# Linear attention with two chunks per step, and the state sums of a chunk as one product

## Chip, cores and metric

The kernel runs on one NeuronCore of a Trainium2 chip. The metric is the device time of one execution in microseconds (us), and the lower one is better. Five queues work beside each other on the core: TensorE (PE in the profile; its weight loads are PEld), VectorE (DVE), ScalarE (ACT), GpSimd (POOL), and SyncE (SP), which here only issues transfers. Each queue takes its instructions in a fixed order, so an instruction that waits holds up all that stand behind it on its queue.

## The reference

A layer of two parts over x with 2048 tokens of width 512, all in float32.

```python
x = x + attn(layernorm(x), Wq, Wk, Wv, Wo)        # 16 query heads, 4 key/value heads, head width 128
x = x + moe(layernorm(x), w_cls, bias, w_gate_up, w_down)   # 64 scores, 8 picked, 32 real experts

# attn: rotary embedding on q and k, then qf = elu(q) + 1, kf = elu(k) + 1, and per head, token by token:
state = state + kf[:, None] * v[None, :]          # 128 x 128
z     = z + kf
out   = (qf @ state) / (qf @ z + 1e-6)
```

The attention is linear: a running 128x128 sum `state` per key/value head takes the place of a softmax over all earlier tokens. The change lies in this part alone, and in the memory that it uses.

## The kernel before, in words

**Tiling.** The 2048 tokens are four blocks (`sb`) of 512; a block has four chunks (`c`) of P = 128 tokens, and a chunk two halves (`a`) of T = 64. There are G = 4 groups (`g`), one for each key/value head, with R = 4 query heads each. Inside a half, attention is computed as masked scores times values; what came earlier enters through the running state, which is therefore needed at the start of each half.

**A block.** `norm_block` normalises the 512 tokens and transposes them to `xT`. `values` makes v for each chunk (L271, one 128x512 PSUM tile, copied by ACT at L274). `project(sb, g)` makes k (L305) and four q (L317) for a group. `rope_feature` (L282 to L288) turns each 128x512 PSUM tile into features: six VectorE instructions and one exponential on ACT. `project` also makes the denominators: a running sum of k (L309), four products with q (`qz`, L325), 16 small matmuls (`pd`, L328), a reciprocal (L331, L332). The reciprocal row is stored to DRAM (L333) and read back once per chunk as `rds`, spread over all 128 partitions (L337, 256 KB per chunk, 512-byte pieces). `by_token` transposes k of the group to `kk` (L294).

**`attend(sb, g, c)`** works on one chunk:
- the scores of both halves (L355): each fills 64 of the 128 PSUM partitions, shown as tile 128*64;
- the sums of k times v (L361), twice: over the first half alone (64 rows, tile 64*128), and over the whole chunk (128*128);
- VectorE adds both to the old state (L366) and masks the scores (`at`, L370);
- for each half, state times q (L376, 128*128) and values times masked scores (L379, 64 rows, 64*128) go into one PSUM tile `po`, one bank for each half;
- VectorE multiplies `po` by `rds` into `oT` (L381).

When group 3 of a block is reached, `output` multiplies `oT` of all 16 heads by Wo, chunk by chunk (`px`, L391), and `route` and `list_further` pick experts for the finished tokens. The second part, the experts, begins after the last block.

**Order.** The loop at the end of the attention writes, for each group, first `project` of the next group and then `attend` of this one, four chunks. A scheduler then places the instructions on each queue, so work of two groups is mixed. It keeps the data dependencies and the limits of the pools: two PSUM buffers `p_pj` for k, q, v and output products; two buffers `p_sc` for scores and sums; one buffer for each `po`; three for `rds` (`rdp`); two for the rotary tables `cs` and `sn` (`blk`), of which the next block's pair is loaded one block ahead; one value tile `va` per chunk.

These are the lines that set how far ahead a reciprocal can be read back, with the names used below:

```python
rdp = ph.enter_context(tc.tile_pool(name="rdp", bufs=NC - 1))      # NC = 4
...
for c in range(NC):
    t = rdp.tile([P, R, P], F32, tag="rds", name=f"rds_{sb}_{g}_{c}")
    nc.sync.dma_start(out=t, in_=recip[sb][g][:, c, :].unsqueeze(0).to_broadcast([P, R, P]))
```

Of the kernel before, what the change touches and what calls it, by code (L numbers as in the profile page):

```python
# [9 lines left out]
F32 = mybir.dt.float32  # L10
# [3 lines left out]
ALU = mybir.AluOpType  # L14
AX = mybir.AxisListType
PSUM = bass.MemoryType.PSUM
DRAM = bass.MemoryType.DRAM

P = 128
# [3 lines left out]
G = 4  # L23
R = H // G
# [28 lines left out]
def linattn_moe(  # L53
# [121 lines left out]

    with ExitStack() as ph:
        wts = ph.enter_context(tc.tile_pool(name="wts", bufs=1))
        blk = ph.enter_context(tc.tile_pool(name="blk", bufs=2))
        xnp = ph.enter_context(tc.tile_pool(name="xnp", bufs=1))
        qkp = ph.enter_context(tc.tile_pool(name="qkp", bufs=2))  # L180
        zp = ph.enter_context(tc.tile_pool(name="zp", bufs=1))
        rdp = ph.enter_context(tc.tile_pool(name="rdp", bufs=NC - 1))
        rowp = ph.enter_context(tc.tile_pool(name="rowp", bufs=NC))
        vap = ph.enter_context(tc.tile_pool(name="vap", bufs=NC))
        otp = ph.enter_context(tc.tile_pool(name="otp", bufs=G))
        stp = ph.enter_context(tc.tile_pool(name="stp", bufs=2))
        tmp = ph.enter_context(tc.tile_pool(name="tmp", bufs=2))
        sml = ph.enter_context(tc.tile_pool(name="sml", bufs=2))
        p_tr = ph.enter_context(tc.tile_pool(name="p_tr", bufs=1, space=PSUM))
        p_pj = ph.enter_context(tc.tile_pool(name="p_pj", bufs=2, space=PSUM))  # L190
        p_sc = ph.enter_context(tc.tile_pool(name="p_sc", bufs=2, space=PSUM))
        p_o = ph.enter_context(tc.tile_pool(name="p_o", bufs=1, space=PSUM))
        p_ms = ph.enter_context(tc.tile_pool(name="p_ms", bufs=1, space=PSUM))

# [50 lines left out]
        def norm_block(sb):  # L245
# [17 lines left out]
                nc.scalar.copy(xT[:, :, ts(c, P)], pt)  # L263
            return xT

        def values(sb, c, xT):

            pv = p_pj.tile([P, G, HD], F32, tag="pj", name=f"pv_{sb}_{c}")
            pvf = pv.rearrange("p g d -> p (g d)")
            for k in range(KD):  # L270
                nc.tensor.matmul(pvf, lhsT=xT[:, k, ts(c, P)], rhs=wv[:, k, :],  # L271
                                 start=(k == 0), stop=(k == KD - 1))
            va = vap.tile([P, G, HD], F32, tag="va", name=f"va_{sb}_{c}")
            nc.scalar.copy(va, pv)  # L274
            return va

        def rope_feature(dst, ps, sb, name):

# [61 lines left out]

        state = [None] * G

        def attend(sb, g, c, proj, kk, va, oT):


            kT, qT, rds = proj
            n = f"{sb}_{g}_{c}"
            halves = range(P // T)
            half = [slice(c * P + a * T, c * P + (a + 1) * T) for a in halves]
            old = state[g]  # L350
            psk = p_sc.tile([P, R * T + 2 * HD], F32, tag="sc", name=f"psk_{n}")
            psc = psk[:, : R * T].rearrange("p (r t) -> p r t", r=R)
            pst = psk[:, R * T :].rearrange("p (a d) -> p a d", a=2)
            for a in halves:
                nc.tensor.matmul(psc[ts(a, T)], lhsT=kT[:, half[a]], rhs=qT[:, :, half[a]],  # L355
                                 start=True, stop=True)

            n_new = 2 if sb < NSB - 1 or c < NC - 1 else 1
            for a in range(n_new):
                to = slice(0, (a + 1) * T)  # L360
                nc.tensor.matmul(pst[:, a], lhsT=kk[to, c], rhs=va[to, g, :], start=True, stop=True)  # L361
            new = stp.tile([P, 2, HD], F32, tag=f"st{g}", name=f"state_{n}")
            if old is None:
                nc.vector.tensor_copy(new, pst)
            else:
                nc.vector.tensor_tensor(new[:, :n_new], pst[:, :n_new],  # L366
                                        old[:, 1:].to_broadcast([P, n_new, HD]), ALU.add)
            state[g] = new
            at = tmp.tile([P, R, T], F32, tag="at", name=f"at_{n}")
            nc.vector.tensor_tensor(at, psc, causal.unsqueeze(1).to_broadcast([P, R, T]), ALU.mult)  # L370
            pos = []
            for a in halves:
                po = p_o.tile([P, R, T], F32, tag=f"o{a}", name=f"po_{n}_{a}")
                before_half = (old[:, 1] if old is not None else None, new[:, 0])[a]
                if before_half is not None:
                    nc.tensor.matmul(po, lhsT=before_half, rhs=qT[:, :, half[a]], start=True, stop=False)  # L376
                pos.append((po, before_half is None))
            for a, (po, first) in enumerate(pos):
                nc.tensor.matmul(po, lhsT=va[ts(a, T), g, :], rhs=at[ts(a, T)], start=first, stop=True)  # L379
            for a, (po, first) in enumerate(pos):  # L380
                nc.vector.tensor_tensor(oT[:, :, half[a]], po, rds[c][:, :, ts(a, T)], ALU.mult)  # L381

        def output(sb, c, oTs, between=None):

# [19 lines left out]
        def route(ch, xw):  # L404
# [16 lines left out]
            nc.vector.reciprocal(sm, sm)  # L421
            nc.vector.tensor_scalar(sc, sc, sm, None, ALU.mult)

            sb_ = sml.tile([P, EZ], F32, tag="sbias", name=f"sbias_{ch}")
            nc.vector.tensor_tensor(sb_, sc, bias_r, ALU.add)
            t8 = sml.tile([P, TOPK], F32, tag="t8", name=f"t8_{ch}")
            nc.vector.max(out=t8, in_=sb_)
            rest = sml.tile([P, EZ], F32, tag="rest", name=f"rest_{ch}")
            nc.vector.match_replace(out=rest, in_to_replace=t8, in_values=sb_, imm_value=-3.0e38)
            sel = sml.tile([P, EZ], F32, tag="sel", name=f"sel_{ch}")  # L430
            nc.vector.tensor_tensor(sel, sb_, rest, ALU.not_equal)
# [18 lines left out]
            nc.vector.tensor_copy(pos, pp)  # L450
            if ch >= LISTED:

                free = sml.tile([P, E], F32, tag="hi", name=f"free_{ch}")
                nc.vector.tensor_scalar(free, sel[:, :E], -float(NONE), float(NONE), ALU.mult, ALU.add)
                nc.vector.tensor_tensor(free, pos, free, ALU.add)
                here = tmp.tile([P, E, SL], BF16, tag="rb", name=f"here_{ch}")
                ph_ = p_ms.tile([P, NQ, 2], F32, tag="ms", name=f"ph_{ch}")
                for i in range(2):
                    es = slice(i * E // 2, (i + 1) * E // 2)
                    nc.vector.tensor_tensor(here[:, es],  # L460
                                            free[:, es].unsqueeze(2).to_broadcast([P, E // 2, SL]),
                                            places.unsqueeze(1).to_broadcast([P, E // 2, SL]), ALU.is_equal)
                    for q in range(i * NQ // 2, (i + 1) * NQ // 2):
                        nc.tensor.matmul(ph_[:, q, :],
                                         lhsT=here[:, Q * q : Q * (q + 1), :].rearrange("p e s -> p (e s)"),
                                         rhs=tok2[:, ch, :], start=True, stop=True)
                nc.vector.tensor_tensor(held, held, ph_, ALU.add)

            hi = sml.tile([P, E], F32, tag="hi", name=f"hi_{ch}")
            nc.vector.tensor_scalar(hi, pos, float(C2), float(P * NCOL - 1), ALU.is_ge, ALU.mult)  # L470
            mi = sml.tile([P, E], F32, tag="mi", name=f"mi_{ch}")
            nc.vector.scalar_tensor_tensor(mi, pos, float(SL), off_2, ALU.is_ge, ALU.mult)
            ad = sml.tile([P, E], F32, tag="ad", name=f"ad_{ch}")
            nc.vector.scalar_tensor_tensor(ad, pos, -float(NCOL), off_e, ALU.mult, ALU.add)
            nc.vector.tensor_tensor(hi, hi, mi, ALU.add)
            nc.vector.tensor_tensor(ad, ad, hi, ALU.add)
            ok = sml.tile([P, E], F32, tag="ok", name=f"ok_{ch}")
            nc.vector.scalar_tensor_tensor(ok, pos, float(CAP), sel[:, :E], ALU.is_lt, ALU.mult)
            nc.vector.tensor_tensor(ad, ad, ok, ALU.mult)
            a8 = sml.tile([P, TOPK], F32, tag="a8", name=f"a8_{ch}")  # L480
# [20 lines left out]
        for sb in range(NSB):  # L501
# [2 lines left out]
                blocks[sb + 1] = load_block(sb + 1)  # L504
            for g in range(G):
                if g == 0:
                    vas = [values(sb, c, xTs[sb]) for c in range(NC)]
                if g + 1 < G:
                    projs[sb, g + 1] = project(sb, g + 1, xTs[sb])
                elif not last:  # L510
                    xTs[sb + 1] = norm_block(sb + 1)
                    projs[sb + 1, 0] = project(sb + 1, 0, xTs[sb + 1])
                if last and g == G - 1:
                    for i in range(2):
                        load_pair(i)
                oT = otp.tile([P, R, SB], F32, tag="oT", name=f"oT_{sb}_{g}")
                oTs[sb, g] = oT
                kk = by_token(sb, g, projs[sb, g][0])
                for c in range(NC):
                    attend(sb, g, c, projs[sb, g], kk, vas[c], oT)  # L520
                    if g == G - 1:
                        if c != 1 and waiting:
                            route_and_list(*waiting.pop(0))
                        if c >= 1:
                            waiting.append((sb * NC + c - 1,
                                            output(sb, c - 1, [oTs[sb, i] for i in range(G)])))
# [20 lines left out]

        pc = p_ms.tile([P, E], F32, tag="ms", name="pc")
        nc.tensor.matmul(pc, lhsT=ones, rhs=selcum, start=True, stop=True)
        big = sml.tile([P, 2, 2, E // 2], F32, tag="big", name="big")  # L550
        for i, n in enumerate((SL, C2)):
            nc.vector.tensor_scalar(big[:, i].rearrange("p a b -> p (a b)"), pc, float(n) + 0.5, None,
                                    ALU.is_ge)
# [296 lines left out]
```

## Time and profile before

| | us |
|---|---|
| median of 3 runs (lowest, highest) | 1238.45 (1237.87, 1241.02) |
| the profiled execution, whole | 1237.05 |
| its span, first to last instruction | 1235.3 |
| PE busy in the span | 1050.5 (85%) |
| DVE busy | 637.9 (52%) |
| ACT, POOL busy | 130.2, 219.7 |
| PE clock granted, mean | 0.933 |

The attention takes about the first 900 us. A block has a stage of values and the first `project` (33.3 us in the second block), two stages of `attend` beside `project` (33.7 and 33.3), a third with the next block's normalisation (35.8), and one with the last group and the output products (80.7). The rest of the span is the experts. These stages run from the first `values` product (L271) or the first transposes of `by_token` (L294) of a group to those of the next. A share of busy time is a mean over stages, so the stages are looked at one by one.

### The profile page before, as it was taken

How to read it: one execution, taken by the hardware profiler on the slowest of the kernel's cores; microseconds unless marked ns; L12 is line 12 of the kernel's file. 1: busy time of each engine (PE TensorE's matmuls, PEld its weight loads, DVE VectorE, ACT ScalarE, POOL GpSimd, SP SyncE). 2: the span in 40 equal slices, each digit the busy share in tenths (PEclk: the TensorE clock that was granted, in tenths of full speed). 3: DMA queues.
4: the chain of work that ended last, by engine and by line, in shares of the span. 5: the costliest groups of instructions: out<-in, count | busy, mean ns of one | idle time of the engine just before them, and what ended most of it. 6: DMA issues, size and time to landing. Idle time of an engine off the chain costs nothing. (4 is left out here: it accounts for less than half of the span.)

```text
span 1235.3 us, 13580 instructions
## 1 busy us (share of the span) xinstructions
PE 1050.5 (85%) x4410; PEld 530.9 (43%) x4410; DVE 637.9 (52%) x1553; ACT 130.2 (11%) x256; POOL 219.7 (18%) x254
## 2 busy tenths in 40 slices
PE   5999999999999899999999999999737765672772
PEld 2444444444444444444444444444312554441440
DVE  4888874358888435888843388834322111110110
ACT  1111110011121001112100111100011100110000
POOL 4000001430000343000034200023353121211211
PEclk9999999999999999999999999999967877786887
DMA  9411212100121210012321112340572484967224
GB/s 346 151 16 33 69 49 55 52 26 13 34 77 40 60 52 27 13 35 58 75 61 52 61 45 67 102 59 27 167 254 74 109 273 149 319 187 235 45 39 156
DMA packets 90840, 116.26 MB, mean 94 GB/s; under 512 B 12493, under 2 KB 47309, under 8 KB 90672
## 3 DMA queue, kind: packets, MB, share of 16 engines
q1 hardware_dynamic: 74640, 93.53, 25.5%
q0 software_dynamic: 10336, 12.51, 5.2%
q10 hardware_dynamic: 5760, 8.92, 2.0%
q8 instruction: 55, 0.90, 0.3%
q14 instruction: 49, 0.40, 0.1%
HBM read 101.35 MB, written 20.96 MB: 99 GB/s over the span
## 5 line engine op out<-in xcount | busy, mean ns | idle before, releaser
L317 PE MATMUL pq<-xT,wq 128*128 128x512 f32 x512 | 230.3, 599 | 10.1 <-DVE rb_q L284 10.1
L391 PE MATMUL px<-wo,oT 128*128 128x512 f32 x512 | 232.4, 599 | 0.0
L166 POOL DMA_INDIRECT slots<-tok,ai x120 | 117.6, 980 | 501.5 <-DVE ai L485 468.9
L317 PEld LDWEIGHTS pq<-xT,wq 128*128 128x128 f32 x512 | 94.4, 190 | 138.5 <-issue 107.3
L391 PEld LDWEIGHTS px<-wo,oT 128*128 128x128 f32 x512 | 93.9, 191 | 98.1 <-issue 97.6
L728 PE MATMUL pu<-xeT,gu 128*128 128x224 f32 (+1 forms) x352 | 69.4, 367 | 11.0 <-DVE xeT L656 9.7
L376 PE MATMUL po<-qT,state 128*128 128x256 f32 x248 | 76.8, 402 | 2.2 <-DVE oT L381 1.9
L728 PEld LDWEIGHTS pu<-xeT,gu 128*128 128x128 f32 x352 | 65.4, 230 | 15.4 <-issue 13.1
L393 DVE TENSOR_TENSOR x<-px,x 128x512 f32<-128x512 f32 x16 | 11.1, 692 | 113.6 <-PE px L391 98.8
L381 DVE TENSOR_TENSOR oT<-po,rds 128x256 f32<-128x256 f32 x128 | 50.1, 414 | 33.7 <-PE po L379 18.8
L305 PE MATMUL pk<-xT,wk 128*128 128x512 f32 x128 | 63.5, 627 | 0.7 <-ACT xT L263 0.7
L242 POOL TENSOR_TENSOR lnr<-lnv,mhalf 128x1 f32<-128x1 f32 (+1 forms) x20 | 13.3, 664 | 255.0 <-DVE lnv L240 228.8
L271 PE MATMUL pv<-wv,xT 128*128 128x512 f32 x128 | 57.7, 598 | 0.0
L361 PE MATMUL psk<-va,kk 64*128 64x128 f32 (+1 forms) x248 | 56.7, 323 | 0.0
L287 ACT ACTIVATE rb_q<-rb_q 128x512 f32<-128x512 f32 x64 | 40.3, 630 | 155.4 <-DVE rb_q L286 155.1
L376 PEld LDWEIGHTS po<-qT,state 128*128 128x128 f32 x248 | 41.2, 189 | 35.6 <-issue 21.7
L379 PE MATMUL po<-at,va 64*128 64x256 f32 x256 | 54.6, 428 | 0.0
L355 PE MATMUL psk<-qT,kT 128*64 128x256 f32 x256 | 50.5, 404 | 0.0
L361 PEld LDWEIGHTS psk<-va,kk 64*128 64x128 f32 (+1 forms) x248 | 36.8, 186 | 31.6 <-issue 23.8
L643 POOL DMA_INDIRECT acc<-y,idx x17 | 25.9, 1524 | 130.0 <-ACTq L778 40.0
L672 PE MATMUL pu_b<-gu,xeT_b 128*32 128x256 f32 x512 | 40.2, 424 | 10.0 <-issue 9.5
L325 DVE TENSOR_TENSOR qz<-qT,zT 128x512 f32<-128x512 f32 x64 | 42.4, 687 | 11.1 <-PE pd L328 10.6
(180 smaller groups left out, 1135.1 us busy)
## 6 DMA issues: line engine op xcount, KB each, us to landing
gu<-in_wgu_dram SPq DMA_DIRECT2D x32, 1024.0 KB
rds<-recip SPq DMA_DIRECT2D x64, 256.0 KB
dn<-in_wdn_dram SPq DMA_DIRECT2D x32, 512.0 KB
rows<-xw ACTq DMA_DIRECT2D x16, 272.0 KB
xn<-in_x_dram SPq DMA_DIRECT2D x16, 256.0 KB
wq<-in_wqT_dram SPq DMA_DIRECT2D x4, 1024.0 KB
wo<-in_woT_dram SPq DMA_DIRECT2D x4, 1024.0 KB
x<-in_x_dram SPq DMA_DIRECT2D x16, 256.0 KB
```

The costliest lines, as they stand in the source:

```text
L166: nc.gpsimd.indirect_dma_start(out=slots[k][:, :], out_offset=bass.IndirectOffsetOnAxis(ap=ai[:, k : k + 1], axis=0), in_=tok[:, ch : ch + 1],
L271: nc.tensor.matmul(pvf, lhsT=xT[:, k, ts(c, P)], rhs=wv[:, k, :], start=(k == 0), stop=(k == KD - 1))
L305: nc.tensor.matmul(pk, lhsT=wk[:, k, ts(g, HD)], rhs=xT[:, k, :], start=(k == 0), stop=(k == KD - 1))
L317: nc.tensor.matmul(pq, lhsT=wq[g][:, k, ts(r, HD)], rhs=xT[:, k, :], start=(k == 0), stop=(k == KD - 1))
L325: nc.vector.tensor_tensor(qz, qT[:, :, cc], zT[:, cc].unsqueeze(1).to_broadcast([P, R, P]), ALU.mult)
L355: nc.tensor.matmul(psc[ts(a, T)], lhsT=kT[:, half[a]], rhs=qT[:, :, half[a]], start=True, stop=True)
L361: nc.tensor.matmul(pst[:, a], lhsT=kk[to, c], rhs=va[to, g, :], start=True, stop=True)
L376: nc.tensor.matmul(po, lhsT=before_half, rhs=qT[:, :, half[a]], start=True, stop=False)
L379: nc.tensor.matmul(po, lhsT=va[ts(a, T), g, :], rhs=at[ts(a, T)], start=first, stop=True)
L381: nc.vector.tensor_tensor(oT[:, :, half[a]], po, rds[c][:, :, ts(a, T)], ALU.mult)
L391: nc.tensor.matmul(px, lhsT=oTs[h // R][:, h % R, ts(c, P)], rhs=wo[h // R][:, h % R, :], start=(h == 0), stop=(h == H - 1))
L728: nc.tensor.matmul(pu[:, a, :m], lhsT=weights[e][0][:, k, a, c, :], rhs=xeT[:, k, :m], start=(k == 0), stop=(k == KD - 1))
```

## The change

Pools: rotary tables one buffer in place of two, `rds` two in place of three, scores one buffer of a whole bank (two chunks) and the sums one bank of their own (`p_st`), in place of two shared ones. The value tiles are made once, with each value held twice: in slot 1 all 128 rows, in slot 0 the first 64 rows with zeros below, which GpSimd writes once at the start. `values` copies into both slots. `attend` takes two chunks: four score products, then one product of 256 columns for each chunk that yields both sums, two state additions, two maskings, four products with the state, four with the values, four multiplications by `rds`. Some small tiles of `route` get one buffer (`sbias`, `rest`, `hi`, `mi`, `ad`, `ok`, `big`), not shown.

```diff
-        blk = ph.enter_context(tc.tile_pool(name="blk", bufs=2))
+        blk = ph.enter_context(tc.tile_pool(name="blk", bufs=1))
-        rdp = ph.enter_context(tc.tile_pool(name="rdp", bufs=NC - 1))
+        rdp = ph.enter_context(tc.tile_pool(name="rdp", bufs=2))
-        vap = ph.enter_context(tc.tile_pool(name="vap", bufs=NC))
+        vap = ph.enter_context(tc.tile_pool(name="vap", bufs=1))
-        p_sc = ph.enter_context(tc.tile_pool(name="p_sc", bufs=2, space=PSUM))
+        p_sc = ph.enter_context(tc.tile_pool(name="p_sc", bufs=1, space=PSUM))
+        p_st = ph.enter_context(tc.tile_pool(name="p_st", bufs=1, space=PSUM))
...
+        vas = [vap.tile([P, G, 2, HD], F32, name=f"va_{c}") for c in range(NC)]
+        for va in vas:
+            nc.gpsimd.memset(va[T:, :, 0, :], 0.0)
         def values(sb, c, xT):
...
-            nc.scalar.copy(va, pv)
+            nc.scalar.copy(vas[c][:, :, 1, :], pv)
+            nc.scalar.copy(vas[c][:T, :, 0, :], pv[:T])
...
-        def attend(sb, g, c, proj, kk, va, oT):
+        def attend(sb, g, c0, proj, kk, oT):
...
+            psc = p_sc.tile([P, 2, R, T], F32, tag="sc", name=f"psc_{n}")
+            for i in chunks:
+                for a in halves:
+                    nc.tensor.matmul(psc[ts(a, T), i], lhsT=kT[:, half[i][a]], rhs=qT[:, :, half[i][a]],
+                                     start=True, stop=True)
-            for a in range(n_new):
-                to = slice(0, (a + 1) * T)
-                nc.tensor.matmul(pst[:, a], lhsT=kk[to, c], rhs=va[to, g, :], start=True, stop=True)
+            pst = p_st.tile([P, 2, 2, HD], F32, tag="st", name=f"pst_{n}")
+            for i in chunks:
+                nc.tensor.matmul(pst[:, i], lhsT=kk[:, c0 + i], rhs=vas[c0 + i][:, g], start=True, stop=True)
...
+            for i in chunks:
+                for a in halves:
+                    if seen[i][a] is not None:
+                        nc.tensor.matmul(po[a][:, i], lhsT=seen[i][a], rhs=qT[:, :, half[i][a]],
+                                         start=fresh[a], stop=False)
+                        fresh[a] = False
+            for i in chunks:
+                for a in halves:
+                    nc.tensor.matmul(po[a][:, i], lhsT=vas[c0 + i][ts(a, T), g, 1, :], rhs=ats[i][ts(a, T)],
+                                     start=False, stop=(i == 1))
+            for i in chunks:
+                for a in halves:
+                    nc.vector.tensor_tensor(oT[:, :, half[i][a]], po[a][:, i], rds[c0 + i][:, :, ts(a, T)],
+                                            ALU.mult)
...
                 for c in range(NC):
-                    attend(sb, g, c, projs[sb, g], kk, vas[c], oT)
+                    if c % 2 == 0:
+                        attend(sb, g, c, projs[sb, g], kk, oT)
```

## Prediction before the run

> **What bounds the kernel now.** I read the page's busy shares first, then the busy time stage by stage (windows), then the order of time on TensorE, then the waits. In the stage table the columns are window and length, then PE, PEld, DVE, ACT and POOL busy (instructions), PE clock, DMA share, GB/s.
>
> ```profile
> 285.70:319.40 33.70, 33.51 (x142) 15.72 (x141) 29.34 (x54) 3.93 (x7) 0.00 (x0) 1.00 0.17 34
> 319.40:352.70 33.30, 32.80 (x141) 15.37 (x140) 29.07 (x54) 3.92 (x7) 0.00 (x0) 1.00 0.14 34
> ...
> 388.50:469.20 80.70, 76.95 (x281) 37.36 (x280) 34.83 (x132) 4.54 (x9) 25.21 (x27) 1.00 0.16 44
> ```
>
> Through the attention PE is busy 95 to 99%, so PE is the bound. But in the first two stages shown (`attend` beside `project`; eight such "dense" stages in the run, 270.0 us by their limits) DVE is busy 29.1 of 33.3 us: only 4.2 us are free. In the third, DVE has room.
>
> A busy PE is no price, since matmuls overlap. I take prices from differences of starts (columns: start, us, engine):
>
> ```profile
> 332.37 0.65 PE L355 MATMUL psk<-qT,kT 128*64 128x256 f32 x4
> 332.95 0.90 PE L361 MATMUL psk<-va,kk 64*128 64x128 f32 x4
> 333.69 1.03 PE L376 MATMUL po<-qT,state 128*128 128x256 f32 x4
> 334.65 0.70 PE L379 MATMUL po<-at,va 64*128 64x256 f32 x4
> 335.28 1.12 PE L305 MATMUL pk<-xT,wk 128*128 128x512 f32 x2
> 336.24 1.03 PE L376 MATMUL po<-qT,state 128*128 128x256 f32 x4
> ```
>
> A float32 product is two records. The four L361 records take 333.69-332.95 = 0.74 us (0.83 where another tile shape follows, as from 321.11 to 321.94). Four L376 records take 0.96. Record by record: a full-array record of 512, 256, 128 columns costs 429, 216, 109 ns; a change of tile shape costs some 93 ns before and 104 after. A pair of score halves (L355) takes 0.58, one half alone also 0.58; a pair of L379 takes 0.63. With these pitches and the order of instructions, PE's attention sums to 853 us; the trace has 892, so 39 are waits.
>
> The last view is the reading back of `rds`:
>
> ```profile
> 363.59 0.38 SPq L337 DMA_DIRECT2D rds<-recip  x1
> ...
> 371.50 0.76 DVE L381 TENSOR_TENSOR oT<-po,rds 128x256 f32<-128x256 f32 x2 [2.66 <-DMA rds<-recip]
> ```
>
> ```profile
> 807.34 9.40 SPq L337 DMA_DIRECT2D rds<-recip  x4
> ...
> 815.59 0.76 DVE L381 TENSOR_TENSOR oT<-po,rds 128x256 f32<-128x256 f32 x2 [5.13 <-DMA rds<-recip]
> ...
> 819.51 0.42 DVE L381 TENSOR_TENSOR oT<-po,rds 128x256 f32<-128x256 f32 x1 [0.64 <-DMA rds<-recip]
> ```
>
> One load takes 371.50-363.59 = 7.9 us from issue to use; the landing events give 7.7 to 8.1 for most. Of three loads issued within 1 us, the first lands after 7.9 to 8.2 and the second some 11 to 12 us after the first issue. Today three buffers hide this: only the fourth chunk waits for a buffer.
>
> **What the Trainium skill says.** "TensorE: Matmul & The Clock Gate", Back-to-back issue gap, gives N/2.4 + 2.5 ns for a product of N columns; two passes of 256 make 216 ns, which is this trace's pitch. The same page, Why this matters for your kernels, says a product with few rows costs as much alone as a full one: agreed, L361's 64-row records have pitches of 213 and 202 ns, its 128-row records 213 and 205. "PSUM — Partial Sum Buffer", PSUM bank collisions, wants accesses of two engines to a bank kept apart in time; so both sums of a pair must be done before the first state addition. "DMA: Bandwidth & Descriptors", Bandwidth, has 6.15 us for 1 MB issued from GpSimd; 256 KB in 512-byte pieces takes 7.9 us here, and the trace decides.
>
> **The change, part by part.**
>
> (1) *PE, -37.0 us.* The 64 first-half products go: 64 x 0.415 = -26.6. The 60 full ones of 128 columns (0.218) become 64 of 256 (0.432): +14.6. Runs of the full shape fall from 160 to 60 in the built order, at 0.197 a run: -19.7. Fewer and longer runs of scores: -3.3; of L379: -3.8; `pd` is split more: +1.8. That is -20.0 in the eight dense stages, -10.7 where group 3 is near (third stage and output stage of three blocks), -6.6 in the tail after the last `project`, +0.3 elsewhere. Nowhere does the trace show a 128-row product of 256 columns with `kk`; L376 has that shape. If it cost two old ones (0.74), 20 us would be lost; if it hid its switch, 6 won. I take L376's price.
>
> (2) *DVE, 0 instructions.* The two state additions, two maskings and four multiplications of a pair are as many as before. So where PE gets shorter, DVE becomes the limit.
>
> (3) *`rds` with two buffers.* The loads of chunks 2 and 3 now wait for the multiplications of chunks 0 and 1. I walked a dense stage (second block, group 1) down both queues with these prices. From the first transposes: PE has scores, sums and part of the next `pk` done at 5.1; DVE, still on the last q, gives the first sums at 4.9 and the second mask at 7.2; PE waits 0.8 for it. Chunk 0's multiplications end at 10.9, so its buffer is reloaded and lands at 18.9. Chunk 1's end at 12.4; its reload is the second of two. Behind the multiplications of chunks 2 and 3 on DVE stand the exponential's input, the scan and the first q (L282 to L284), which frees a `p_pj` buffer 5.2 us after the last multiplication; PE's third q product waits for that. Without any wait for `rds` the stage takes 32.3; with the second load landing 9.6 after the first issue, 34.2; with 11.7, 36.3. The same walk of the stage before gives 33.8 where the trace has 33.3, so I take off 0.45: 31.85, 33.75, 35.85. The second load can't land before 1.5 (its later issue) + 7.9 = 9.4, and the trio above says up to 11.7. I take 9.6: the loads are 1.5 us apart, and in the trace what was issued 1.5 to 2.1 us behind a load landed 0.2 to 0.8 after the one ahead. Eight dense stages: 8 x 33.75 = 270.0, so **0 in place of -20.0**.
>
> (4) *Group 3 and tail.* In the third stage, the first state product of group 3 (in the order ahead of the next block's k) waits for chunks 2 and 3's `po`, so for their `rds`: 1.8 us x 3 = +5.4. Transposes for the router stalled 3.3 and 3.0 us in two blocks; two chunks ahead of them cover this, though the next one shows 1.3 more in each block: -2.7. Tail: the same `rds` wait once, +0.6 over today's stall of 2.2 us there, and +1.0 for a transpose. Together -10.7 - 6.6 + 5.4 - 2.7 + 1.6 = -13.0.
>
> (5) *Small ones.* Four value memsets (0.5 us each by the 128x544 one) and the other constants now all precede `lnr` on POOL, which has 3.4 free us there: +0.4. The second ACT copy of `values` (16 x 0.6): ACT is 11% busy; uncovered, it would delay the next PSUM buffer by 0.6 of the 3.4 us of a product: 0. Single rotary tables: the loads wait for the last q's L284, about 4 us into the third stage, and are needed 12 us later; on SP they stand ahead of chunk 2's `rds`, whose own wait ends later: 0; if the cover fails, the k of three blocks waits, +1 to +3 each. Single small tiles: writer and reader are both DVE in order: 0. POOL's lists and ACT's stores keep their order.
>
> Sum: 0 - 13.0 + 0.3 + 0.4 = -12.3. Against the profiled execution, 1237.05 - 12.3 = 1224.8; the median stands 1.4 higher, so **1226 us**.
>
> **The rivals.**
> - *A: as above*, second load 9.4 to 10.2 behind: 1224 to 1234 by 12 waits x 0.8. Chance 0.45.
> - *B: slower, `rds` latency decides.* Each of 12 waits (8 dense, 3 third stages, tail) grows with the landing of the second load. At 11.7, 2.1 us later than I took: 12 x 2.1 = +25, 1251; at 11.4, 1248. It turns into a loss past 9.6 + 12.3/12 = 10.6. For it: the line at 819.51. Against: there the loads were 0.45 us apart, and a third shared the engines. Chance 0.25 for over 10.9; 0.15 lies between A and B, 1234 to 1242.
> - *C: no wait on `rds`,* since DVE arrives late anyway or the second load overlaps wholly: 8 x (33.75-31.85) + 5.4 + 0.6 = 21 us more, 1205. For it: no line; against: the 7.9. Chance 0.15.
> - *D: the wide product is no cheaper* than the two old ones: +20 on PE, but in dense stages DVE hides half, so some 1236; inside the middle case.
>
> **How the numbers follow.** 0.3% (3.7 us) is about what a measurement of this kernel can tell from no change. Faster: C, nearly all of A and some of the middle, 0.62. Same: 0.15. Slower: B with a remnant of D, 0.23. The range 1208 to 1249 leaves out the lower half of C and the upper end of B. The likeliest case's own range is 1220 to 1234.
>
> **What would show it right or wrong.** Right: one sums row of 128x256 at 0.43 to 0.48 us a product; PE busy lower by some 30 us; the waits of `oT` on `rds` up from 14.7 us in 7 to over 20 in some 15 or more; dense stages still near 33.7 with PE idle before q products (L317 before) and waiting for DVE. Wrong: dense stages of 32 or less (C), of 35 or more (B), or idle PE ahead of the state additions, which the walk puts at 0.8 us a stage.

## The result and the profile after

| | us | ratio to before (95% interval) |
|---|---|---|
| before, median of 4 runs | 1238.62 | |
| changed, median of 4 runs | 1291.18 | 1.0419 (1.0391 to 1.0448) |
| profiled span, before and after | 1235.3, 1291.1 | |

The change makes the kernel 4.2% slower. The forecast was 1226, with a range up to 1249. The page first: busy times, the granted clock in 40 slices, then the two groups whose idle time grew (busy us, mean ns of one; idle time just before them and what ended most of it).

```profile
PE 1046.7 (81%) x4290; PEld 544.0 (42%) x4290; DVE 638.4 (49%) x1553; ACT 137.7 (11%) x272; POOL 222.0 (17%) x258
...
PEclk9998899999998999988999998898968777877786
...
L322 PE MATMUL pq<-xT,wq 128*128 128x512 f32 x512 | 249.4, 643 | 45.3 <-DVE rb_q L289 42.8
...
L394 DVE TENSOR_TENSOR oT<-po,rds 128x256 f32<-128x256 f32 x128 | 49.0, 418 | 87.5 <-DMA rds<-recip 78.9
```

The same two lines of the kernel before, its clock row, and its wait for `rds` from the list of waits (us in total, times, longest):

```profile
PEclk9999999999999999999999999999967877786887
L317 PE MATMUL pq<-xT,wq 128*128 128x512 f32 x512 | 230.3, 599 | 10.1 <-DVE rb_q L284 10.1
L381 DVE TENSOR_TENSOR oT<-po,rds 128x256 f32<-128x256 f32 x128 | 50.1, 414 | 33.7 <-PE po L379 18.8
```

```profile
DVE oT L381 <- DMA rds<-recip: 14.7, 7, 5.1
```

PE's and DVE's shares of the span both fell, so it is waiting that grew. VectorE stands 78.9 us for `rds`, where it stood 14.7 before. PE idles 45.3 us ahead of q products (10.1 before), and each record of a q product takes 643 ns where it took 599. The clock row has eights in it from the fourth slice on; before, it had nines all through the first 29. Something makes TensorE run slower inside the attention.

The stage table says where (columns as in the prediction: window, length, busy of PE, PEld, DVE, ACT, POOL, PE clock, DMA share, GB/s):

```profile
292.80:331.60 38.80, 33.41 (x134) 16.70 (x133) 29.46 (x55) 3.92 (x7) 0.00 (x0) 0.91 0.18 29
331.60:366.90 35.30, 32.34 (x134) 16.16 (x133) 29.51 (x54) 3.93 (x7) 0.00 (x0) 0.95 0.15 32
411.20:492.10 80.90, 75.23 (x264) 37.59 (x263) 34.61 (x130) 4.55 (x9) 25.19 (x27) 0.98 0.18 44
```

The same two dense stages took 33.7 and 33.3 before, at clock 1.00. All eight dense stages sum to 304.1 us (270.0 before): **+34.1**. Third and output stages of three blocks sum to 361.0 (346.0): **+15.0**. The attention after the last `project` is 5.2 longer (103.1 to 108.3 us, up to the last router transpose), the experts 2.7 longer, start and `values` 1.2 shorter. Together these make the whole 55.8 us.

How one stage loses its time is seen on three queues of the changed kernel, in order of time. First SyncE and VectorE (start, us, line, what; in brackets the idle time and what ended it):

```profile
303.19 1.89 SPq L342 DMA_DIRECT2D rds<-recip  x2
```

```profile
311.01 0.42 DVE L394 TENSOR_TENSOR oT<-po,rds 128x256 f32<-128x256 f32 x1 [1.50 <-DMA rds<-recip]
315.06 1.09 DVE L394 TENSOR_TENSOR oT<-po,rds 128x256 f32<-128x256 f32 x3 [3.63 <-DMA rds<-recip]
...
328.34 0.69 DVE L287 TENSOR_TENSOR qT<-pq,cs 128x512 f32<-128x512 f32 x1 [1.85 <-PE pq L322]
```

And TensorE:

```profile
309.63 7.13 PE L322 MATMUL pq<-xT,wq 128*128 128x512 f32 x16
321.92 9.81 PE L322 MATMUL pq<-xT,wq 128*128 128x512 f32 x16 [5.16 <-DVE rb_q L289]
331.58 0.60 PE L299 MATMUL pk<-ident,kT 128*128 128x128 f32 x4
```

The two reloads are issued at 303.19 and 304.70. The first is used at 311.01, the second at 315.06, 11.9 us after the first issue. VectorE waits 1.50 + 3.63. Behind the wait stand the k features and the first q (L287 to L289), which free the buffer of the third q product: PE idles 5.16 us. Then sixteen records that took 7.13 us take 9.81. The trace's clock record has 0.5 from 320.53 to 327.36; such a stretch is called half clock below. The second half of the q products is therefore late, and VectorE waits for it once more (1.85). Over the eight dense stages VectorE waits 37.6 us for `rds` (3.4 before) and 11.7 us for such late q products. Half clock within the attention: 85 us after, 3.4 before.

The price of the wide product, for the line L361 that the prediction showed:

```profile
333.12 1.13 PE L364 MATMUL pst<-va,kk 128*128 128x256 f32 x4
334.09 0.59 PE L385 MATMUL po<-qT,state 128*128 128x256 f32 x2
```

Two products with one change of shape take 334.09 - 333.12 = 0.97 us; record by record the pitch is 216 ns, so 0.432 a product.

### The profile page after: what moved, and what is told of

Same layout as the page of the kernel before. It is cut to its first block, busy times and chain, and to the rows that moved or that the text cites. A ratio compares the mean times of both kernels' runs of the same rounds, so it can differ in the third digit from the quotient of the medians.

```text
span 1291.1 us, 13361 instructions
## 1 busy us (share of the span) xinstructions
PE 1046.7 (81%) x4290; PEld 544.0 (42%) x4290; DVE 638.4 (49%) x1553; ACT 137.7 (11%) x272; POOL 222.0 (17%) x258
## 5 line engine op out<-in xcount | busy, mean ns | idle before, releaser
L322 PE MATMUL pq<-xT,wq 128*128 128x512 f32 x512 | 249.4, 643 | 45.3 <-DVE rb_q L289 42.8
L322 PEld LDWEIGHTS pq<-xT,wq 128*128 128x128 f32 x512 | 103.3, 206 | 186.1 <-issue 124.6
L394 DVE TENSOR_TENSOR oT<-po,rds 128x256 f32<-128x256 f32 x128 | 49.0, 418 | 87.5 <-DMA rds<-recip 78.9
L385 PE MATMUL po<-qT,state 128*128 128x256 f32 x248 | 67.1, 392 | 19.4 <-DVE oT L394 10.9
L385 PEld LDWEIGHTS po<-qT,state 128*128 128x128 f32 x248 | 46.3, 193 | 40.3 <-DVE state L372 16.0
L390 PE MATMUL po<-at,va 64*128 64x256 f32 x256 | 51.6, 424 | 0.0
L287 DVE TENSOR_TENSOR qT<-pq,cs 128x512 f32<-128x512 f32 x64 | 43.8, 685 | 12.8 <-PE pq L322 11.9
L293 DVE SCALAR_TENSOR_TENSOR qT<-qT,rb_q 128x512 f32<-128x512 f32 x64 | 44.3, 693 | 4.6 <-ACT rb_q L292 2.1
L359 PE MATMUL psc<-qT,kT 128*64 128x256 f32 x256 | 45.6, 396 | 0.0
L288 DVE TENSOR_TENSOR rb_q<-pq,sn 64x512 f32<-64x512 f32 x64 | 44.4, 693 | 1.7
L688 PE MATMUL pu_b<-gu,xeT_b 128*32 128x256 f32 x512 | 37.6, 415 | 8.7 <-issue 8.6
```

The lines of the kernel that those rows point to most:

```text
L288: nc.vector.tensor_tensor(b[:hh], ps[hh:], sn[hh:], ALU.mult)
L293: nc.vector.scalar_tensor_tensor(dst, dst, 0.0, b, ALU.max, ALU.add)
L322: nc.tensor.matmul(pq, lhsT=wq[g][:, k, ts(r, HD)], rhs=xT[:, k, :], start=(k == 0), stop=(k == KD - 1))
L359: nc.tensor.matmul(psc[ts(a, T), i], lhsT=kT[:, half[i][a]], rhs=qT[:, :, half[i][a]], start=True, stop=True)
L385: nc.tensor.matmul(po[a][:, i], lhsT=seen[i][a], rhs=qT[:, :, half[i][a]], start=fresh[a], stop=False)
L390: nc.tensor.matmul(po[a][:, i], lhsT=vas[c0 + i][ts(a, T), g, 1, :], rhs=ats[i][ts(a, T)], start=False, stop=(i == 1))
```

## The experiments

**Theory:** TensorE's work got cheaper as forecast, but two `rds` buffers put two transfers, one after the other, into every stage; VectorE stands, TensorE idles, and then its clock is halved. **Rivals:** the paired order or the wide product is itself dearer; the half clock is an onlooker; VectorE bounds the dense stages anyway. The kernels ran on more than one chip; the kernel before took 1227.65 to 1238.24 us beside them, so ratios and stage lengths are compared. The ratio also holds the experts, whose length moves from 330 to 347 us between these kernels with no part of the change in them; small differences are therefore read from the stages. "Dense" is the sum of the eight dense stages, "third + output" that of both stages in three blocks, all in us of the profiled execution:

| kernel | ratio to before (95%) | dense | third + output | `rds` waits in dense |
|---|---|---|---|---|
| before | 1 | 270.0 | 346.0 | 3.4 |
| changed | 1.0419 | 304.1 | 361.0 | 37.6 |
| a_rd4 | 0.9804 (0.9761 to 0.9847) | 251.7 | 347.8 | none |
| b_rd2 | 1.0381 (1.0327 to 1.0435) | 300.5 | 363.4 | 37.1 |
| a_fill | 1.0368 (1.0315 to 1.0421) | 309.2 | 350.2 | 45.0 |
| a_two | 0.9862 (0.9814 to 0.9910) | 259.4 | 341.9 | none |
| a_one | 0.9967 (0.9953 to 0.9982) | 267.1 | 348.7 | 15.5 |
| b_wide | 0.9914 (0.9887 to 0.9941) | 266.1 | 342.0 | 0.7 |
| a_list | 0.9794 (0.9746 to 0.9842) | 251.7 | 346.2 | none |
| a_list2 | 0.9769 (0.9733 to 0.9805) | 251.7 | 337.2 | none |

### a_rd4: four buffers for `rds`

```diff
-        rdp = ph.enter_context(tc.tile_pool(name="rdp", bufs=2))
+        rdp = ph.enter_context(tc.tile_pool(name="rdp", bufs=NC))
...
-                qz = tmp.tile([P, R, P], F32, tag="qz", name=f"qz_{sb}_{g}_{c}")
+                qz = tmp.tile([P, R, P], F32, tag="rb", name=f"qz_{sb}_{g}_{c}")
...
```

> The changed kernel with four rds buffers in place of two (the space comes from letting qz and xrT share the two rb buffers; TensorE's and VectorE's order is the same as in the changed kernel). Theory (the reloads into two buffers are the whole loss: the second lands 11 to 14 us after the first is issued, VectorE stands, TensorE idles 3 to 6 us and then gets half the clock for 3.4 to 10 us): no oT<-rds waits, dense stages 32 to 33 us instead of 38, hardly any half clock before the router's last part, 1203 to 1222 us. Rival 1 (the wide product or the pairing itself is dearer on TensorE, the rds wait only fills the same hole): dense stages stay over 36, 1270 or more. Rival 2 (VectorE bounds the dense stages anyway): they come back only to the 33.7 of before, 1225 to 1240.

Measured: 0.9804 (1205.8 us, with the kernel before at 1227.7 beside it; 1214 where before takes 1238.6). Its second block's dense stages:

```profile
276.60:308.20 31.60, 30.98 (x134) 15.61 (x133) 29.00 (x54) 3.92 (x7) 0.00 (x0) 1.00 0.16 36
308.20:339.80 31.60, 31.17 (x133) 15.42 (x132) 28.76 (x54) 3.92 (x7) 0.00 (x0) 1.00 0.15 36
```

PE is busy 31.0 of 31.6 us at the full clock, and with TensorE's and VectorE's instructions in the same order VectorE has no wait for `rds` in any dense stage. The whole loss and more lay in the two buffers; rivals 1 and 2 fall. PE is busy 1017.6 us in all, 32.9 less than before. One thing stays open: four buffers are one more than before had, and some of the gain over the kernel before may be that buffer's, since before waits 14.7 us for `rds` (3.4 in the dense stages). No run has the kernel before with four.

### b_rd2: the kernel before with two buffers

```diff
-        rdp = ph.enter_context(tc.tile_pool(name="rdp", bufs=NC - 1))
+        rdp = ph.enter_context(tc.tile_pool(name="rdp", bufs=2))
```

> The kernel before with two rds buffers in place of three, nothing else (one chunk at a time, two products for the sums). Theory (two buffers alone make the loss): chunks 2 and 3 wait some 4 us longer than today's chunk 3, TensorE idles over 2.5 us ahead of a q product and the half clock appears; dense stages 36 to 39, 1255 to 1285 us. Rival (it is the pairing: with one chunk at a time the two reloads start apart and land singly, 7.9 us each): dense stages up by 0 to 1.5, 1239 to 1252.

Measured: 1.0381, nearly the loss of the whole change, without pairs and without wide products. One dense stage, and VectorE's two waits in it:

```profile
293.40:330.80 37.40, 33.64 (x141) 15.58 (x140) 29.29 (x54) 3.92 (x7) 0.00 (x0) 1.00 0.16 30
```

```profile
313.01 0.76 DVE L381 TENSOR_TENSOR oT<-po,rds 128x256 f32<-128x256 f32 x2 [2.51 <-DMA rds<-recip]
317.52 0.76 DVE L381 TENSOR_TENSOR oT<-po,rds 128x256 f32<-128x256 f32 x2 [1.60 <-DMA rds<-recip]
```

The rival's premise was right for the starts and its conclusion wrong: in the dense stages the reloads start 2.7 to 3.3 us apart, but chunk 3's cannot start before chunk 1 is multiplied, and it lands 7.9 to 12.0 us after its issue, so its data still come late. Half clock in the dense stages is only 13.7 us here (54.6 in the changed kernel), and yet they sum to 300.5. The four that have none, like the one shown at clock 1.00, still lose 3.1 to 3.7 us each. So the wait alone makes a loss of this size, and in this kernel the halved clock is the smaller part. One detail was expected otherwise: TensorE's longest idle times in the dense stages (up to 3.1 us) stand ahead of products with `state`; ahead of q products they are at most 2.2.

### a_fill: idle time filled with products

```diff
+                if r == 2 and g >= 2:
+                    fill = p_ms.tile([P, 2 * P], F32, tag="ms", name=f"fill_{sb}_{g}")
+                    for k in range(7):
+                        nc.tensor.matmul(fill, lhsT=wq[g][:, k % KD, ts(r, HD)], rhs=xT[:, k % KD, : 2 * P],
+                                         start=True, stop=True)
```

> The changed kernel with seven idle 256-column products (3.0 us at the full clock, result not used) put on TensorE ahead of the third q product of groups 2 and 3, where it idles 3 to 6 us in the eight dense stages. It adds work and takes none away. Theory (the half clock after the idle time costs about 1.9 us a dense stage): the half clock vanishes from most dense stages, each 1 to 2.5 us shorter, 1270 to 1285 us. Rival (the half clock costs nothing, VectorE being the bound while it lasts): 1290 to 1298, as the changed kernel or longer.

Measured: 1.0368 on the whole, and dense stages that sum to more than without. As a whole this is inconclusive, because the scheduler moved other products from the second dense stage on, and the waits for `rds` grew to 45.0. The first dense stage, ahead of any move, is clean (the added code shifts lines by five):

```profile
95.44 3.19 PE L324 MATMUL fill<-xT,wq 128*128 128x256 f32 x14
100.47 7.13 PE L327 MATMUL pq<-xT,wq 128*128 128x512 f32 x16 [1.84 <-DVE rb_q L289]
107.44 0.60 PE L299 MATMUL pk<-ident,kT 128*128 128x128 f32 x4
```

The sixteen records take 7.13 again, no half clock follows, and this stage is 35.3 us where it was 38.4: -3.1, about half of the 6.8 us of half clock that it had. VectorE's waits for late q products fall from 11.7 to 2.2 us over the eight stages. So the half clock does cost time there; what it costs over all stages can't be read from this run.

### a_two: two chunks at a time alone

```diff
...
-                nc.tensor.matmul(pst[:, i], lhsT=kk[:, c0 + i], rhs=vas[c0 + i][:, g], start=True, stop=True)
+                for a in halves:
+                    to = slice(0, (a + 1) * T)
+                    nc.tensor.matmul(pst[:, i, a], lhsT=kk[to, c0 + i], rhs=vas[c0 + i][to, g, :],
+                                     start=True, stop=True)
...
```

> Two chunks at a time alone: the sums stay two products (64 and 128 rows) with values held once, four rds buffers, rotary tables double. Theory: as a_rd4 without the gain of the wide product, which is 12 us of columns and some of its switches of tile shape on TensorE, partly hidden beside VectorE: 5 to 20 us above a_rd4, still below the kernel before. Rival (the wide product is no cheaper than the two): equal to a_rd4 within 4 us.

Measured: 0.9862. Dense stages of 32.4 us on average, 7.7 us more in sum than in a_rd4, as the theory has it; but third and output stages are 5.9 us shorter than in a_rd4, so the two intervals overlap and the whole time does not decide against the rival. That the kernel with the wide product loses near group 3 most of what it wins in the dense stages was not forecast. In the output stages of blocks 1 and 2 (counted from 0), TensorE idles 3.7 us ahead of a product with `state` in a_rd4, with half clock behind it, and 2.1 us in a_two, without; a_list2 below finds what makes this idle time.

### a_one: one reload a wait

```diff
+                if c == NC - 1:
+                    rds.append(rds[2])
+                    continue
                 t = rdp.tile([P, R, P], F32, tag="rds", name=f"rds_{sb}_{g}_{c}")
```

> The changed kernel with two rds buffers, but chunk 3 of each group multiplies by chunk 2's reciprocals, so that its own read-back is left out: one reload a wait in place of two. Theory (most of the loss is the second reload, which lands 11 to 14 us after the first one's issue; the first one alone lands after 7.7 to 8.9 and would make VectorE wait some 1.5 us a stage): oT<-rds waits below 2.5 us a dense stage, TensorE's idle time ahead of the third q product under 2.5 us, no half clock there, dense stages 32 to 34.5 us; 0.99 to 1.01 of the kernel before. Rival (any reload inside the stage costs it the whole 6.5 us, because VectorE's order stops at the first): dense stages over 36, 1.03 or more.

Measured: 0.9967, dense stages 32.5 to 35.0 us. The wait and the stage that is left:

```profile
299.29 1.42 DVE L397 TENSOR_TENSOR oT<-po,rds 128x256 f32<-128x256 f32 x4 [1.71 <-DMA rds<-recip]
```

The wait goes from 1.50 + 3.63 to 1.71; over the eight stages it is 0.8 to 3.3 us, one of them above the 2.5 that was expected, and the lone reload lands after 7.9 to 9.6 us. Two of the eight stages exceed the forecast's 34.5 (34.6; 35.0 with 3.4 us of half clock). Of the 52.4 us between the changed kernel and a_rd4 in the dense stages, 37.0 hang on the second reload. The rival falls.

### b_wide: the wide product alone

```diff
...
-            for a in range(n_new):
-                to = slice(0, (a + 1) * T)
-                nc.tensor.matmul(pst[:, a], lhsT=kk[to, c], rhs=va[to, g, :], start=True, stop=True)
...
+            nc.tensor.matmul(pst, lhsT=kk[:, c], rhs=va[:, g], start=True, stop=True)
...
```

> The kernel before (one chunk at a time, three rds buffers) with the wide product alone: values held twice, rotary tables single, qz and xrT in the rb buffers. Theory (128x256 at 0.43 us against 0.415 + 0.218 for the two, and a change of tile shape fewer): 13 to 25 us off TensorE, partly hidden beside VectorE in the dense stages; 0.985 to 0.995 of the kernel before. Rival (the wide product is no cheaper in place): within 0.3% of the kernel before.

Measured: 0.9914, within the expectation. One chunk at a time the product wins 3.9 us in the dense stages; pairing with four `rds` buffers (a_two) wins 10.6, both (a_rd4) 18.3. The last two hold the 3.4 us that before waits for `rds` there. Rotary tables held once are in this kernel too, and cost nothing that shows: its third stages are 35.4 us where before has 38.5, 35.8, 35.8.

### a_list and a_list2: what holds up the second state addition

a_rd4 won nothing in third and output stages (347.8 against 346.0). In the output stages of blocks 1 and 2 TensorE idles 3.7 us ahead of a product with `state`. TensorE in the first of them, then the order of time around it on GpSimd and VectorE:

```profile
408.53 1.22 PE L385 MATMUL po<-qT,state 128*128 128x256 f32 x2 [3.69 <-DVE state L372]
```

```profile
406.98 0.59 POOL L243 TENSOR_TENSOR lnr<-lnv,mhalf 128x1 f32<-128x1 f32 x1
407.60 0.55 DVE L415 TENSOR_SCALAR xw<-x,mv,lnr 128x512 f32<-128x512 f32 x1 [4.05 <-POOL lnr L243]
408.06 0.42 DVE L372 TENSOR_TENSOR state<-pst,state 128x256 f32<-128x256 f32 x1
```

VectorE stands at `xw` for GpSimd's `lnr`; GpSimd is busy with eight list transfers, one every 1.28 us, and the pair's second state addition is queued behind `xw`. Both kernels put the transfers behind `lnr`; a_list does so for chunks that are routed beside an `output` of their own block, a_list2 (shown) for all.

```diff
-                            route_and_list(*waiting.pop(0))
+                            found.append(route(*waiting.pop(0)))
...
                                             output(sb, c - 1, [oTs[sb, i] for i in range(G)])))
+                            with tc.issue_after(rstd_of.last.ins):
+                                while found:
+                                    list_further(*found.pop(0))
...
             while waiting:
-                route_and_list(*waiting.pop(0))
+                found.append(route(*waiting.pop(0)))
+            while last and found:
+                list_further(*found.pop(0))
```

> a_rd4 with the router's list transfers issued on GpSimd behind the next chunk's lnr (1/sqrt of the variance) instead of ahead of it. Theory (the gain that was forecast where group 3 is near is lost to VectorE standing at xw for lnr behind eight indirect transfers, with the second state addition of the pair behind it: TensorE idles 3.7 us in two blocks and then has half the clock): these gaps go, output stages 76 to 79 us instead of 81 to 82, 0.3 to 1% below a_rd4. Rival (VectorE or the router is late there anyway): within 0.2% of a_rd4.

Measured: a_list gives 0.9794, the same as a_rd4, and the 3.69 us stand where they stood. This says nothing on the theory, since the edit missed the place: the eight transfers there belong to a chunk of the block before, and stayed ahead of `lnr`.

> As a_list, and the list transfers of the last two chunks of a block too go behind lnr of the next block's first output chunk. a_list left these ahead of it, and there the 3.7 us idle time stood: VectorE waited at xw for lnr behind eight transfers, with the second state addition behind it. Theory: the gaps of 3.7 us in blocks 1 and 2 go, and the half clock after them (6.8 us each) with them; TensorE is the bound there, so the output stages of 81.5 and 81.1 us lose 3.7 + some 3 each, to 74 to 76 us; 0.5 to 1.2% below a_list. Rival 1 (the half clock costs nothing): 3.7 each, 77.5 us. Rival 2 (the wait moves to another place, such as 16 transfers in a row ahead of the following lnr): over 80 us.

Measured: a_list2 gives 0.9769. The line at `xw` and the next stall of TensorE:

```profile
402.04 0.61 DVE L415 TENSOR_SCALAR xw<-x,mv,lnr 128x512 f32<-128x512 f32 x1 [0.39 <-POOL lnr L243]
...
425.57 0.63 PE L422 MATMUL prt<-ident,xw 128*128 128x128 f32 x4 [2.98 <-DVE xw L415]
```

The idle time and the half clock after it are gone; the output stages fall from 81.5 and 81.1 (a_list) to 77.2 and 76.3 us. That is less than forecast, because 16 transfers in a row now make the next `lnr` late (2.98 and 2.07 us of new idle time): the second rival is right in part. The length is also close to rival 1's 77.5, but rival 1 had no new idle time in it. From the sum, 81.5 - 77.2 = 4.3 = 3.69 - 2.98 + 3.6, and 4.8 = 3.67 - 2.07 + 3.2 in the other block: as an estimate, 6.8 us of half clock cost TensorE 3.2 to 3.6 us where it is the bound. a_list2 is the fastest kernel here, 2.3% below the one before; its interval overlaps those of a_rd4 and a_list.

## Why the prediction was wrong

**Step (1), PE: right.** The product costs 0.432 us as taken, PE's busy time in a_rd4 is 32.9 us lower (about 30 was forecast), and without waits for `rds` the dense stages take 251.7 us, where the walk had 8 x 31.85 = 254.8. A reading aside: two passes of 256 columns at N/2.4 + 2.5 ns make 218 ns, and 216 only if the 2.5 is counted once; the sum used the trace's 216, so nothing hangs on it. In the changed kernel itself PE's busy time fell by 3.8 only, because records at half clock last longer.

**Step (2), DVE unchanged: right.**

**Step (3), the waits: the step that failed.** It put the dense stages at 0 and they lost 34.1 us. The mechanism, the queue behind it and the point of turning (10.6 us) were there; a term was mis-sized, and one was missing. The split between them is an estimate.
- *Landing of the second reload.* Taken: 9.6 us after the first issue. Measured by the landing events of the eight dense pairs: 11.0 to 14.3, mean 11.94. By the walk's own slope (2.1 us a stage for 2.1 us of landing) this is 8 x 2.34 = 18.7 us. The choice rested on what landed 0.2 to 0.8 us after the load ahead of it. In the trace these are not second loads: they are the 64 KB stores of the reciprocal row (L333, 0.2 to 0.5 behind a load), and third loads of trios, issued 1.5 us behind a second that was itself late (0.7). Every second load of a trio before landed 10 to 12 us after its own issue, and that was the row to take. In the dense pairs of the changed kernel the second load's first piece lands after 4.7 to 7.0 us, much as the first load's (5.4 to 7.2); it is its last pieces that come late.
- *Half clock, missing.* The walk put TensorE's idle time at its own length. The Trainium skill, "TensorE: Matmul & The Clock Gate", Why this matters for your kernels, wants no idle time above about 3 us between bursts of products; the prediction used that page for pitches and passed this line over. From 70 to 860 us of the changed kernel, all fourteen idle times of TensorE of 2.56 us or more were followed by half clock, and none of the three between 1.5 and 1.7. VectorE's waits for late q products (none in the dense stages before or in a_rd4) put it at 11.7 us of the dense stages.
- The remaining 3.7 us, under 0.5 a stage, are not traced to a cause.

**Rival B, right in sign, mechanism and place,** and too small: its 1251 had the landing at 11.7, near the truth, without the clock and with the gains of step (4). It had a chance of 0.25 where the rows of the trios spoke for it.

**Step (4), group 3 and tail: wrong by 23.0 and 12.9 us.** Third and output stages were to gain 13.4 and lose 5.4 to `rds`. The loss to `rds` was 13.2 (361.0 against 347.8 in a_rd4): waits of some 8 us in each third stage, and half clock after them. The gain did not come even without `rds` waits (+1.8 in a_rd4): the step priced TensorE and let the pair's second state addition wait for PE alone, while on its own queue it stands behind `xw`. With that stall moved, a_list2 gains 8.8. The tail was to gain 5.0 and lost 7.9: VectorE waits there 16.5 us for `rds` (5.8 before). Of the 7.9, 2.7 lie in the experts, which move by more than this between kernels.

**Step (5): right.** No wait for `cs` or `sn` shows in the changed kernel, and the four `values` stages take 134.4 us (134.5 before) with the second ACT copy.

**What would show it:** L364 and the `rds` waits did as listed (26 waits, 78.9 us); dense stages over 35 were named as the sign of B. Idle PE ahead of the state additions, put at 0.8 us a stage, was not seen in the dense stages.

## What to carry to other kernels

Price a buffer that is taken away with the landing of the last transfer that the waiting instruction needs, read from transfers issued in the same grouping; a second one in flight can double the visible wait. When a wait leaves TensorE idle for some 2.5 us or more, expect half clock behind it (all fourteen times in the changed kernel, most times in the others), and add half of its length where TensorE is the bound. When instructions of two steps are put together, look at what stands between them on the slower engine's queue: the second state addition was late because of a GpSimd list, not of a product.

## What the runs showed of the hardware

- Half clock comes in stretches of 3.41, 6.83 or 10.24 us, which fits the free-running window of 3413 ns that the Trainium skill, "TensorE: Matmul & The Clock Gate", Part 1, gives. Idle times of 4.7 to 5.8 us brought 6.8, one of 6.23 brought 10.24. Between 1.5 and 3.3 us it went either way in these kernels, so that page's limit of about 3 us is not sharp here: 2.12 brought 3.4 us in a_fill and 1.52 brought 10.24 in b_rd2, 3.22 brought none in a_one.
- A lone 256 KB load in 512-byte pieces lands after 7.7 to 9.6 us (before and a_one). Of two issued 1.5 us apart in the changed kernel's dense stages, the first lands after 7.7 to 8.9, so it is not later for it, and the second lands 9.5 to 12.8 after its own issue.
